# Dividing the side work of an attention kernel over two steps, and spreading the ones-products of its softmax sums

## The chip, the cores and the metric

The kernel runs on one core of one Trainium2 chip. The metric is the device time of one execution in microseconds (us). The median of three runs before the change is 3438.81 us.

## The reference, cut to what matters

Eight graphs ("frames") of 2048 nodes with 256 channels go through one attention layer with an adjacency mask, eight heads of 32 channels, a feed-forward part, and three layer norms:

```
qkv = einsum('fnc,ck->fnk', x, w_qkv); q, k, v = split(qkv, 3)      # F=8, N=2048, C=256, H=8, D=32
scores = einsum('fnhd,fmhd->fhnm', q, k) / sqrt(D)
scores = where(adj > 0, scores, -1e9)
attn = softmax(scores, axis=-1)
t = einsum('fhnm,fmhd->fnhd', attn, v).reshape(F, N, C)
x1 = layernorm(x + t)
h = relu(x1 @ w1 + b1)
out = layernorm(x + layernorm(x1 + h @ w2 + b2))
```

All data is float32.

## The kernel before, in words

**Steps and groups.** The list `items` has 1024 entries (f, qc, g, mb): frame, chunk of 512 queries, one of two halves of the heads (four heads each), and one of 16 blocks of 128 keys. The main loop takes one item per *step*. The 16 steps of one (f, qc, g) are a *group*; there are 64 groups, eight to a frame. At step t the program issues, in this order: at most one piece of *side work* (`advance`), the exponentials of item t+1, the scores of item t+2, the values product of item t, and the adding-up of item t. I call the place between the values product of one step and the scores of the next step the *slot* of that step.

**What a step holds on each engine.** TensorE (PE): four score matmuls, one for each head (L215), and four values matmuls (L234). VectorE (DVE): two additions of the mask to the scores, which also move them out of PSUM (L218). ScalarE (ACT): one exponential over 128x2048 (L222). The scores live in three PSUM tiles `s0` to `s2`; a step takes two of them in turn, so the scores of the next step need the first mask addition of this one.

**The sums of the softmax** are not made by the matmul that makes the values. The 16 exponential tiles of a group are first added: blocks 0, 3, 6, 8, 11, 13, 15 by GpSimd (POOL, L256, six additions), blocks 1, 4, 7, 10 and 2, 5, 9, 12 in two chains by accumulating DMAs that POOL issues (L253, six DMAs of 1 MB; each waits for the one before it in its chain), and block 14 stays alone. Then `denominator` multiplies the four remaining tiles by ones (L292): four sets of four matmuls, in the order block 14, first chain, second chain, POOL's tile. It runs inside the next group: two sets in the slot of block 3 and two in the slot of block 4. Then come a copy (L294), four transposes (L299) and reciprocals on DVE (L304 to L306).

**The rest of the side work** are generators in the list `fill`, sorted by due time. `turn` transposes the rows of the next frame and makes its queries (L152, L172), `project` makes its keys (L172) and values (L197), `outcome` divides by the sums (L328), and `tail` does layer norm, feed-forward (L394, L405, L415), layer norm, residual and layer norm, with bn_stats on DVE (L263, L264), scaling on ACT (L274) and products on POOL (L397, L399, L339, L341). A generator yields a positive number to sleep so many steps, or `BANK` when it wants the one free PSUM bank (of `x0` and `x1` one holds the running output of the group, the other serves side work). `advance(t, 1)` grants one `BANK` per step; after a grant the generator runs to its next yield, so a whole piece is issued in one slot: two matmuls of 128x512 for L172 or L405, eight of 128x128 for L197, four of 128x256 for L415, eight for L292, four transposes for the others. The first step of a group gets no slot.

**POOL's queue** runs in program order: L256, L253 and the tail's instructions stand in it as their steps issued them. A chain DMA that has to wait for the DMA before it holds up everything behind it.

Of the kernel before, what the change touches and what calls it, by code (L numbers as in the profile page):

```python
# [10 lines left out]
F32 = mybir.dt.float32  # L11
# [8 lines left out]
P = 128  # L20
H = 8
D = 32
CH = 512
# [3 lines left out]

SUM_MIN = 1e-25
SUM_MAX = 1e19
BANK, TURNED, ROOM, INPUTS = -1, -2, -3, -10  # L30

MASKED = -57344.0
CODE = -5.0
# [22 lines left out]
def fast_path(ctx, tc, cst, x, adj, out, RS):  # L56
    nc = tc.nc
    F, N, C = x.shape
# [18 lines left out]
    ctx.enter_context(tc.manual_schedule())  # L77

    ident, identb, wqkv, w1s, w2s = cst["ident"], cst["identb"], cst["wqkv"], cst["w1s"], cst["w2s"]
    state = {"pair": 0, "side": None, "turn": 0, "turned": False, "tails": 0}  # L80

    def score_pair():
        i = state["pair"]
# [57 lines left out]

    def queries(f, c, xT):
        for g in range(2):
            yield BANK
            QT[f, c, g] = channels(qp, "qT", xT, g * P)

    def turn_rows(xc, xT):
        for a in range(2):
# [17 lines left out]
        yield from queries(f, c, xT)  # L166
        give(xT)

    def channels(pool, name, xT, k0):
        ps = bank()  # L170
        for a in range(2):
            nc.tensor.matmul(ps, wqkv[:, a, k0:k0 + P], xT[:, a, :], start=(a == 0), stop=(a == 1))  # L172
        t = pool.tile([P, CH], F32, name=name)
        nc.scalar.copy(t, ps)
        return t

    def reload(f, c):
        while (f, c) not in XT:
# [7 lines left out]
    def project(f, c, g, xT=None):  # L186
        if xT is None:
            xT = yield from reload(f, c)
            while len(KT) < (2 * f + g) * NCK + c:
                yield 1  # L190
        yield BANK
        KT[f, c, g] = channels(kp, "kT", xT, C + g * P)
        yield BANK
        ps = bank()
        for j in range(TPC):
            for a in range(2):
                nc.tensor.matmul(ps[:, j * P:(j + 1) * P], xT[:, a, j * P:(j + 1) * P],  # L197
                                 wqkv[:, a, 2 * C + g * P:2 * C + (g + 1) * P], start=(a == 0), stop=(a == 1))
        v = vp.tile([P, TPC, P], F32, name="v")
        nc.scalar.copy(v, ps.rearrange("p (j c) -> p j c", c=P))  # L200
        V[f, c, g] = v
        give(xT)
# [21 lines left out]
    LAST = MB - 1  # L224
# [19 lines left out]
    ALONE = 14  # L244

    ENDED = (13, 15)
    SUM = 4

    def add_up(item):
        f, qc, g, mb = item  # L250
# [29 lines left out]
    def denominator(f, qc, g):  # L280
        grp = (f, qc, g)
        terms = [PT.pop((f, qc, g, ALONE))] + [PT.pop((f, qc, g, chain[0])) for chain in MOVED + (POOLED,)]
        if (f, qc, g) == items[-1][:3]:
            terms[3:3] = [PT.pop((f, qc, g, b)) for b in ENDED]
        yield BANK
        ps = bank()
        for n, term in enumerate(terms):
            if n == 2:
                yield BANK
            for h in range(4):  # L290
                r = D * h
                nc.tensor.matmul(ps[r:r + D, :], cst["ones"], term[:, h, :], start=(n == 0), stop=(n == len(terms) - 1))  # L292
        dT = op.tile([P, CH], F32, name="dT")
        nc.scalar.copy(dT, ps)  # L294
        yield 1
        yield BANK
        ps = bank()
        for j in range(TPC):
            nc.tensor.transpose(ps[:, j * P:(j + 1) * P], dT[:, j::TPC], ident)  # L299
        if g == 0:  # L300
            RC[f, qc] = op.tile([P, TPC, H], F32, name="rc")
        rc = RC[f, qc]
        den = ps.rearrange("p (j c) -> p j c", c=P)[:, :, ::D]
        nc.vector.reciprocal(rc[:, :, 4 * g:4 * g + 4], den)  # L304
        nc.vector.tensor_tensor(RS[:, 0], RS[:, 0], den, ALU.add)
        nc.vector.tensor_tensor(RS[:, 1], RS[:, 1], den, ALU.min)  # L306
        if g == 1:
            begin = items.index((f, qc, g, LAST)) + SUM + 2
            start(begin, outcome(f, qc) if (f, qc) != (F - 1, NCK - 1) else finish(f, qc), begin)

    def outcome(f, qc):
        yield ROOM
        state["tails"] += 1
        xin = x[f, qc * CH:(qc + 1) * CH, :].rearrange("(p j) c -> p j c", p=P)
        y = yp.tile([P, TPC, C], F32, name="y")
        yield from divide(f, qc, y)
        nc.gpsimd.dma_start(y, xin, accum_op=ALU.add)
        begin = items.index((f, qc, 1, LAST)) + SUM + 2
        start(begin + 10, tail(f, qc, y, xin), begin + 26)

    def divide(f, qc, y):
        rc = RC.pop((f, qc))
# [63 lines left out]
    def feed_forward(y):  # L386
        yield TURNED
        state["turned"] = True
        yT = work.tile([P, 2, CH], F32, name="turned")
        for a in range(2):  # L390
            yield BANK
            ps = bank()
            for j in range(TPC):
                nc.tensor.transpose(ps[:, j * P:(j + 1) * P], y[:, j, a * P:(a + 1) * P], ident)  # L394
            nc.scalar.activation(yT[:, a, :], ps, AF.Identity, bias=cst["be1c"][:, a:a + 1], scale=cst["g1c"][:, a:a + 1])
        yield 1
        nc.gpsimd.tensor_tensor(y, y, rows(cst["g1r"]), ALU.mult)  # L397
        yield 1
        nc.gpsimd.tensor_tensor(y, y, rows(cst["be1b2r"]), ALU.add)  # L399
        hT = work.tile([P, 2, CH], F32, name="hT")  # L400
        for d in range(2):
            yield BANK
            ps = bank()
            for a in range(2):
                nc.tensor.matmul(ps, w1s[:, a, d * P:(d + 1) * P], yT[:, a, :], start=(a == 0), stop=(a == 1))  # L405
            nc.scalar.activation(hT[:, d, :], ps, AF.Relu, bias=cst["b1s"][:, d:d + 1], scale=1.0)
        state["turned"] = False
        yield 1
        z = y
        for jj in range(0, TPC, 2):  # L410
            yield BANK
            ps = bank()
            for j in range(jj, jj + 2):
                for d in range(2):
                    nc.tensor.matmul(ps[:, (j - jj) * C:(j - jj + 1) * C], hT[:, d, j * P:(j + 1) * P], w2s[:, d, :],  # L415
                                     start=(d == 0), stop=(d == 1))
            nc.vector.tensor_tensor(z[:, jj:jj + 2, :], ps.rearrange("p (b c) -> p b c", c=C), z[:, jj:jj + 2, :], ALU.add)
# [4 lines left out]
    def start(t, gen, due):  # L422
        fill.append([t, gen, 1, due])
        fill.sort(key=lambda e: e[3])

    def advance(t, banks):
        inputs = True
        for e in list(fill):  # L430
            while e[0] <= t:
                if e[2] == BANK:
                    if not banks:
                        break
                    banks -= 1
                elif e[2] < INPUTS:
                    inputs = inputs and not any(u is not None for u in live[:INPUTS - e[2]])
                    if not inputs:
                        break
                elif e[2] == TURNED and state["turned"] or e[2] == ROOM and state["tails"] == 2:  # L440
                    break
                e[2] = next(e[1], None)
                if e[2] is None:
                    fill.remove(e)
                    break
                if e[2] > 0:
                    e[0] = t + e[2]

    items = [(f, qc, g, mb) for f in range(F) for qc in range(NCK) for g in range(2) for mb in range(MB)]
    LEAD = 2  # L450

# [61 lines left out]
    for t, (f, qc, g, mb) in enumerate(items):  # L513
        if mb == 0 and t:
            state["side"] = 1 - state["side"]
        if g == 1 and mb % 2 and (f + 1 < F or qc + 1 < NCK):
            load_mask(f + (qc + 1) // NCK, (qc + 1) % NCK, mb // 2)
        if f + 1 < F:
            for what, *which in NEXT.get((2 * qc + g, mb), []):
                due = t + MB // 2 if what is turn else items.index((f + 1, 0, which[1], which[0] * TPC)) - LEAD - 1  # L520
                start(t, what(f + 1, *which), due)
        if t == len(items) - MB // 2:
            state["rows"] = take([P, TPC, C], F32)
            nc.sync.dma_start(state["rows"], x[f, qc * CH:(qc + 1) * CH, :].rearrange("(p j) c -> p j c", p=P))
        if mb:
            advance(t, 1)

        if t + 1 < len(items):
            exponentials(items[t + 1])
        if t + LEAD < len(items):  # L530
            nf, _, ng, nmb = items[t + LEAD]
            t0 = t
            while (nf, nmb // TPC, ng) not in V:
                advance(t0, 1)
                t0 += 1
            scores(items[t + LEAD])
        values(items[t])
        add_up(items[t])
        if mb == LAST:
            start(t + SUM, denominator(f, qc, g), t)  # L540
    t = len(items)
    state["side"] = None
    while fill:
        t += 1
        advance(t, 1)


@with_exitstack
# [233 lines left out]
```

## Time and profile before

| what | value |
|---|---|
| three timed runs | 3435.35, 3440.09, 3438.81 us |
| the profiled execution: its own time | 3440.89 us |
| its span in the trace | 3439.1 us |
| busy DVE / ACT / POOL | 2731.0 / 2426.5 / 2586.7 us |
| DVE L218 mask additions | 2048, 1219 ns each |
| ACT L222 exponentials | 1024, 1911 ns each |
| POOL L256 additions | 382, 4898 ns each |
| first values product / end of the span | 94.86 / 3439.1 us |

The page counts an engine as busy while an instruction is in its pipeline; on PE neighbouring matmuls overlap, so the timeline's starts tell more than the durations. A matmul in float32 shows as two records. In the arrows, `[0.41 <-DVE p L218]` behind a row means that its engine was idle for 0.41 us before it, until the DVE instruction of line 218 had released it.

### The profile page before, as it was taken

The numbers are of one execution on the slowest core, as the hardware profiler recorded it, in microseconds if no ns is written. First come the engines' busy times: TensorE is split into PE (matmuls) and PEld (weight loads), VectorE is DVE, ScalarE is ACT, GpSimd is POOL, SyncE is SP. The second block draws the span as 40 slices with busy tenths as digits, with TensorE's granted clock in tenths as the row PEclk, the third lists the DMA queues.
The fourth block names the chain that finished last, engine by engine and source line by source line (L and its number), as shares of the span: only waits on it lengthen the run. The fifth ranks groups of instructions, "written<-read, shape, count | busy, mean of one in ns | idle before, by whom it ended". The sixth has DMA issues, their size and how long they took to land. (4 is left out here: it accounts for less than half of the span.)

```text
span 3439.1 us, 54435 instructions
## 1 busy us (share of the span) xinstructions
PE 3179.1 (92%) x22036; PEld 1038.5 (30%) x22036; DVE 2731.0 (79%) x3203; ACT 2426.5 (71%) x1937; POOL 2586.7 (75%) x1357
## 2 busy tenths in 40 slices
PE   6989999999999999999999999999999999998995
PEld 5222332223322233222332323223332223322222
DVE  4788768887788877888788887888768887689885
ACT  3677767776677767777677776777767777677774
POOL 0577768887688776888678876787777877788885
PEclk8999999999999999999999999999999999999998
DMA  8678768778678777778777777687776787777774
GB/s 309 149 156 173 173 161 174 158 159 200 142 167 184 154 180 153 163 172 181 170 154 170 161 175 178 141 180 172 164 179 140 160 187 167 169 158 154 151 162 99
DMA packets 149298, 575.99 MB, mean 167 GB/s; under 512 B 14608, under 2 KB 67344, under 8 KB 99888
## 3 DMA queue, kind: packets, MB, share of 16 engines
q0 software_dynamic: 64560, 435.85, 63.2%
q1 hardware_dynamic: 83664, 135.30, 11.4%
q8 instruction: 174, 2.85, 0.3%
q10 hardware_dynamic: 816, 1.31, 0.1%
q14 instruction: 84, 0.69, 0.1%
HBM read 131.99 MB, written 37.75 MB: 49 GB/s over the span
## 5 line engine op out<-in xcount | busy, mean ns | idle before, releaser
L218 DVE TENSOR_TENSOR p<-s,mask 128x1024 f32<-128x1024 f32 x2048 | 2410.0, 1219 | 568.5 <-PE s L215 343.9
L222 ACT ACTIVATE p<-p 128x2048 f32<-128x2048 f32 x1024 | 1956.6, 1911 | 484.6 <-DVE p L218 371.2
L256 POOL TENSOR_TENSOR p<-p 128x2048 f32<-128x2048 f32 x382 | 1851.8, 4898 | 385.9 <-ACT p L222 383.4
L215 PE MATMUL s<-qT,kT 32*128 32x512 f32 x8192 | 1169.8, 641 | 184.9 <-DVE p L218 174.6
L234 PE MATMUL x<-p,v 128*32 128x512 f32 x8192 | 1091.8, 605 | 2.3 <-ACT p L222 2.3
L253 POOL DMA_DIRECT2D p<-p x384 | 385.6, 1024 | 376.0 <-DMA p<-p 188.4
L215 PEld LDWEIGHTS s<-qT,kT 32*128 32x128 f32 x8192 | 320.5, 183 | 822.3 <-DVE p L218 756.2
L234 PEld LDWEIGHTS x<-p,v 128*32 128x32 f32 x8192 | 161.1, 108 | 780.1 <-issue 211.5
L172 PE MATMUL x<-in,wqkv 128*128 128x512 f32 x472 | 235.2, 621 | 14.7 <-DMA in<-xd 14.1
L292 PE MATMUL x<-p,ones 128*32 128x512 f32 x2064 | 244.9, 592 | 1.9 <-DMA p<-p 1.9
L274 ACT ACTIVATE y<-y,nb,rs 128x256 f32<-128x256 f32 x372 | 219.0, 590 | 7.1 <-POOL nb L271 7.1
L263 DVE BATCH_NORM_STATS2 st<-y 128x6 f32<-128x256 f32 x372 | 155.4, 418 | 0.0
L172 PEld LDWEIGHTS x<-in,wqkv 128*128 128x128 f32 x472 | 80.2, 189 | 170.9 <-issue 112.7
L294 ACT COPY dT<-x 128x512 f32<-128x512 f32 x64 | 37.4, 585 | 126.3 <-PE x L292 126.3
L415 PE MATMUL x<-w2s,hT 128*128 128x256 f32 x504 | 125.5, 392 | 0.1
L405 PE MATMUL x<-turned,w1s 128*128 128x512 f32 x248 | 123.0, 618 | 0.0
L197 PEld LDWEIGHTS x<-wqkv,in 128*128 128x128 f32 x896 | 104.2, 191 | 47.0 <-issue 41.1
L197 PE MATMUL x<-wqkv,in 128*128 128x128 f32 x896 | 114.9, 281 | 0.0
L292 PEld LDWEIGHTS x<-p,ones 128*32 128x32 f32 x2064 | 66.8, 110 | 156.4 <-issue 151.0
L415 PEld LDWEIGHTS x<-w2s,hT 128*128 128x128 f32 x504 | 90.6, 189 | 62.0 <-issue 50.3
L268 POOL TENSOR_TENSOR rs<-rs,mhalf 128x4 f32<-128x4 f32 x93 | 96.2, 1035 | 7.8
L200 ACT COPY v<-x 128x512 f32<-128x512 f32 x58 | 33.9, 585 | 93.6 <-PE x L197 93.6
(114 smaller groups left out, 1467.6 us busy)
## 6 DMA issues: line engine op xcount, KB each, us to landing
p<-p POOLq DMA_DIRECT2D x384, 1024.0 KB, 10.1
mask<-md SPq DMA_DIRECT2D x248, 128.0 KB, 6.2
y<-in_x_dram POOLq DMA_DIRECT2D x62, 512.0 KB, 6.1
in<-xd SPq DMA_DIRECT2D x59, 512.0 KB, 10.9
p<-in_adj_dram SPq DMA_DIRECT2D x16, 1024.0 KB, 9.6
out_dram<-y SPq DMA_DIRECT2D x31, 512.0 KB, 6.4
in<-in_x_dram SPq DMA_DIRECT2D x29, 512.0 KB, 10.4
xd<-in SPq DMA_DIRECT2D x28, 512.0 KB, 9.2
```

What stands on the lines that cost most here:

```text
L172: nc.tensor.matmul(ps, wqkv[:, a, k0:k0 + P], xT[:, a, :], start=(a == 0), stop=(a == 1))
L197: nc.tensor.matmul(ps[:, j * P:(j + 1) * P], xT[:, a, j * P:(j + 1) * P], wqkv[:, a, 2 * C + g * P:2 * C + (g + 1) * P], start=(a == 0), s ...
L215: nc.tensor.matmul(ps2[half][:, j, :], KT[f, mb // TPC, g][r:r + D, (mb % TPC) * P:(mb % TPC + 1) * P], QT[f, qc, g][r:r + D, :], start=Tr ...
L218: nc.vector.tensor_tensor(pt[:, 2 * half:2 * half + 2, :], ps, MK[f, qc, mb // 2][:, mb % 2, None, :].to_broadcast([P, 2, CH]), ALU.add)
L222: nc.scalar.activation(PT[item], PT[item], AF.Exp, scale=1.0 / math.sqrt(D))
L234: nc.tensor.matmul(O[grp][r:r + D, :], V[f, mb // TPC, g][:, mb % TPC, r:r + D], PT[item][:, h, :], start=(mb == 0), stop=(mb == LAST))
L253: nc.gpsimd.dma_start(PT[f, qc, g, chain[0]], PT.pop(item), accum_op=ALU.add)
L256: nc.gpsimd.tensor_tensor(first, first, PT.pop(item), ALU.add)
L263: nc.vector.bn_stats(st, t[:, j, :])
L274: nc.scalar.activation(t[:, j, :], t[:, j, :], AF.Identity, bias=nb[:, j:j + 1], scale=rs[:, j:j + 1])
L292: nc.tensor.matmul(ps[r:r + D, :], cst["ones"], term[:, h, :], start=(n == 0), stop=(n == len(terms) - 1))
L415: nc.tensor.matmul(ps[:, (j - jj) * C:(j - jj + 1) * C], hT[:, d, j * P:(j + 1) * P], w2s[:, d, :], start=(d == 0), stop=(d == 1))
```

## The change

1. Pieces of two halves (L172 queries and keys, L197, L405, L415) get a `yield MORE` in their middle: the first half runs in one slot, the second in the next step's slot, with the PSUM bank held between them. While a piece is held nobody else gets a bank. If some other generator waits for a bank and is due within eight steps (`SOON`), the held piece is finished at once. It is also finished at once in the last step of a group.
2. The ones-products are offered singly: one set of four matmuls, `MORE`, one set, `HOLD`, one set, `MORE`, one set. `HOLD` is not shortened by a due job, `MORE` is. They begin at block 1 of the next group instead of block 3 (`SUM` 2 instead of 4). Their due time and that of `outcome` become 0, ahead of all else.
3. Small moves: `project` is due seven steps earlier, `tail` may begin three steps earlier (13 steps after the group's last, `2 + 4 + 7`, against 16, `4 + 2 + 10`), and `outcome` at the same step as before.

```
-    def channels(pool, name, xT, k0):
+    def channels(store, pool, name, key, xT, k0):
+        yield BANK
         ps = bank()
         for a in range(2):
+            if a:
+                yield MORE
             nc.tensor.matmul(ps, wqkv[:, a, k0:k0 + P], xT[:, a, :], start=(a == 0), stop=(a == 1))
...
     def project(f, c, g, xT=None):
...
         for j in range(TPC):
+            if j == TPC // 2:
+                yield MORE
             for a in range(2):
                 nc.tensor.matmul(ps[:, j * P:(j + 1) * P], xT[:, a, j * P:(j + 1) * P],
...
-    SUM = 4
+    SUM = 2
...
     def denominator(f, qc, g):
...
         for n, term in enumerate(terms):
-            if n == 2:
-                yield BANK
+            if n:
+                yield HOLD if n == 2 else MORE
             for h in range(4):
...
         if g == 1:
-            begin = items.index((f, qc, g, LAST)) + SUM + 2
-            start(begin, outcome(f, qc) if (f, qc) != (F - 1, NCK - 1) else finish(f, qc), begin)
+            begin = items.index((f, qc, g, LAST)) + SUM + 4
+            start(begin, outcome(f, qc) if (f, qc) != (F - 1, NCK - 1) else finish(f, qc), 0)
...
-        begin = items.index((f, qc, 1, LAST)) + SUM + 2
-        start(begin + 10, tail(f, qc, y, xin), begin + 26)
+        begin = items.index((f, qc, 1, LAST)) + SUM + 4
+        start(begin + 7, tail(f, qc, y, xin), begin + 26)
...
     def feed_forward(y):
...
             for a in range(2):
+                if a:
+                    yield MORE
                 nc.tensor.matmul(ps, w1s[:, a, d * P:(d + 1) * P], yT[:, a, :], start=(a == 0), stop=(a == 1))
...
             for j in range(jj, jj + 2):
+                if j > jj:
+                    yield MORE
                 for d in range(2):
...
-    def advance(t, banks):
+    def resume(e, t):
+        e[2] = next(e[1], None)
+        state["holder"] = e if e[2] in (MORE, HOLD) else None if state["holder"] is e else state["holder"]
+        if e[2] is None:
+            fill.remove(e)
+        elif e[2] > 0:
+            e[0] = t + e[2]
+
+    def advance(t, free=True, finish=False):
         inputs = True
+        if state["holder"]:
+            free = False
+            resume(state["holder"], t)
         for e in list(fill):
-            while e[0] <= t:
+            while e[2] is not None and e[0] <= t and e is not state["holder"]:
                 if e[2] == BANK:
-                    if not banks:
+                    if not free:
                         break
-                    banks -= 1
+                    free = False
...
-                e[2] = next(e[1], None)
-                if e[2] is None:
-                    fill.remove(e)
-                    break
-                if e[2] > 0:
-                    e[0] = t + e[2]
+                resume(e, t)
+        late = any(e[2] == BANK and e[0] <= t and e[3] <= t + SOON for e in fill)
+        while state["holder"] and (finish or late and state["holder"][2] == MORE):
+            resume(state["holder"], t)
+
+    SOON = 8
...
-                due = t + MB // 2 if what is turn else items.index((f + 1, 0, which[1], which[0] * TPC)) - LEAD - 1
+                due = t + MB // 2 if what is turn else items.index((f + 1, 0, which[1], which[0] * TPC)) - LEAD - 8
...
-            advance(t, 1)
+            advance(t, finish=mb == LAST)
...
-            start(t + SUM, denominator(f, qc, g), t)
+            start(t + SUM, denominator(f, qc, g), 0)
```

More of the change, by code (lines that the diff above doesn't have):

```diff
@@ L29 @@
 SUM_MAX = 1e19
-BANK, TURNED, ROOM, INPUTS = -1, -2, -3, -10
+BANK, MORE, HOLD, TURNED, ROOM, INPUTS = -1, -2, -3, -4, -5, -10
 MASKED = -57344.0
@@ L79, in fast_path @@
     ident, identb, wqkv, w1s, w2s = cst["ident"], cst["identb"], cst["wqkv"], cst["w1s"], cst["w2s"]
-    state = {"pair": 0, "side": None, "turn": 0, "turned": False, "tails": 0}
+    state = {"pair": 0, "side": None, "turn": 0, "turned": False, "holder": None, "tails": 0}
     def score_pair():
@@ L143, in queries @@
         for g in range(2):
-            yield BANK
-            QT[f, c, g] = channels(qp, "qT", xT, g * P)
+            yield from channels(QT, qp, "qT", (f, c, g), xT, g * P)
     def turn_rows(xc, xT):
@@ L167, in turn @@
         give(xT)
-    def channels(pool, name, xT, k0):
+    def channels(store, pool, name, key, xT, k0):
+        yield BANK
         ps = bank()
         for a in range(2):
+            if a:
+                yield MORE
             nc.tensor.matmul(ps, wqkv[:, a, k0:k0 + P], xT[:, a, :], start=(a == 0), stop=(a == 1))
-        t = pool.tile([P, CH], F32, name=name)
-        nc.scalar.copy(t, ps)
-        return t
+        store[key] = pool.tile([P, CH], F32, name=name)
+        nc.scalar.copy(store[key], ps)
     def reload(f, c):
@@ L190, in project @@
                 yield 1
-        yield BANK
-        KT[f, c, g] = channels(kp, "kT", xT, C + g * P)
+        yield from channels(KT, kp, "kT", (f, c, g), xT, C + g * P)
         yield BANK
@@ L287, in denominator @@
         for n, term in enumerate(terms):
-            if n == 2:
-                yield BANK
+            if n:
+                yield HOLD if n == 2 else MORE
             for h in range(4):
@@ L533, in fast_path @@
             while (nf, nmb // TPC, ng) not in V:
-                advance(t0, 1)
+                advance(t0, finish=True)
                 t0 += 1
@@ L544, in fast_path @@
         t += 1
-        advance(t, 1)
+        advance(t, finish=True)
 @with_exitstack
```

## The prediction

> **What bounds the kernel now.** I read the page first, then the groups of instructions, the waits, the timeline of PE and that of POOL. Page and groups:
>
> ```profile
> PE 3179.1 (92%) x22036; PEld 1038.5 (30%) x22036; DVE 2731.0 (79%) x3203; ACT 2426.5 (71%) x1937; POOL 2586.7 (75%) x1357
> L215 PE MATMUL s<-qT,kT 32*128 32x512 f32 x8192 | 1169.8, 641 | 184.9 <-DVE p L218 174.6
> p<-p POOLq DMA_DIRECT2D x384, 1024.0 KB, 10.1
> ```
>
> PE is the fullest engine, and nearly all of its later idle time stands before the score matmuls, ended by the mask addition. The waits say how often, and show a second thing, POOL held up by its own chain DMAs:
>
> ```profile
> POOL p L253 <- DMA p<-p: 188.4, 43, 6.2
> PE s L215 <- DVE p L218: 174.6, 359, 1.5
> ```
>
> (Columns: us in all, times, longest.) PE waited 359 times; there are 357 steps without side work in the order of PE's instructions, so the idle time is that of the empty slots. The timeline of PE over five steps (start, length, instruction):
>
> ```profile
> 1634.47 1.07 PE L234 MATMUL x<-p,v 128*32 128x512 f32 x8
> 1635.94 1.14 PE L215 MATMUL s<-qT,kT 32*128 32x512 f32 x8 [0.41 <-DVE p L218]
> 1637.02 1.06 PE L234 MATMUL x<-p,v 128*32 128x512 f32 x8
> 1638.01 1.99 PE L415 MATMUL x<-w2s,hT 128*128 128x256 f32 x8
> 1639.93 1.14 PE L215 MATMUL s<-qT,kT 32*128 32x512 f32 x8
> 1641.01 1.07 PE L234 MATMUL x<-p,v 128*32 128x512 f32 x8
> 1642.00 2.05 PE L197 MATMUL x<-wqkv,in 128*128 128x128 f32 x16
> 1643.98 1.14 PE L215 MATMUL s<-qT,kT 32*128 32x512 f32 x8
> 1645.05 1.06 PE L234 MATMUL x<-p,v 128*32 128x512 f32 x8
> 1645.94 1.90 PE L292 MATMUL x<-p,ones 128*32 128x512 f32 x16
> 1647.77 1.14 PE L215 MATMUL s<-qT,kT 32*128 32x512 f32 x8
> 1648.84 1.06 PE L234 MATMUL x<-p,v 128*32 128x512 f32 x8
> ```
>
> From one L234 to the next is one step. Scores cost 1.07 us and values 1.00, so PE alone needs 2.07. An empty step takes 2.55, a step with a whole piece of L415 3.99, of L197 4.04, of ones 3.79. A whole piece hides DVE completely; an empty step waits 0.4 to 0.5 us for it. Cutting the whole timeline at the L234 starts gives the same by kind: whole L172 or L405 3.98, L415 3.99, L197 4.05, two ones-sets 3.78, transposes 2.65 to 2.86, empty steps other than a group's first 2.60 on average.
>
> The third view is POOL's timeline at the end of a second-half group whose sums fall in the group starting at 1535.18:
>
> ```profile
> 1514.99 0.93 POOL L253 DMA_DIRECT2D p<-p  x1 [0.28 <-issue]
> 1521.20 0.87 POOL L253 DMA_DIRECT2D p<-p  x1 [5.28 <-DMA p<-p]
> 1521.77 4.87 POOL L256 TENSOR_TENSOR p<-p 128x2048 f32<-128x2048 f32 x1
> 1526.26 2.71 POOL L397 TENSOR_TENSOR y<-y,g1r 128x1024 f32<-128x1024 f32 x1
> 1528.58 1.23 POOL L253 DMA_DIRECT2D p<-p  x1
> 1529.19 3.00 POOL L399 TENSOR_TENSOR y<-y,be1b2r 128x1024 f32<-128x1024 f32 x1
> 1531.51 9.82 POOL L256 TENSOR_TENSOR p<-p 128x2048 f32<-128x2048 f32 x2
> ```
>
> The last row ends at 1541.33 with the group's last addition. Its ones-product is the fourth set and runs at about 1548.7, 7 us later: POOL has room now.
>
> **What the Trainium skill says.** "Perfetto Trace Analysis", Optimization Strategy: where the most-contended engine changes over time, interleaving the regimes may help. The trace agrees that there are two regimes, PE-bound steps of 3.98 and DVE-bound steps of 2.55. "DMA: Bandwidth & Descriptors", Issuing engines are not separate DMA queues: all DMAs interleave on the same 16 engines. Here the chain DMAs land 6.8 to 13.9 us after issue (median 10.1), so their landing isn't a constant. "GPSIMD Engine Reference", Elementwise, has 4497 ns for an addition over 2048 floats; the trace shows 4.5 us from start to start of two such additions, so POOL's additions are at their price and won't shrink.
>
> **Part 1, the spreading on PE.** No matmul is added or removed. I counted the slots in the instruction order of both programs. Before: 357 empty, 126 of two ones-sets, 118+62 whole L172 and L405, 61 L415, 56 L197. After: 160 empty; ones 104 single and 74 double; L172 168 halves and 34 whole; L405 44 and 40; L415 64 and 29; L197 14 and 49. So 84+22+32+7 = 145 pieces are divided, 52 ones-pairs are, and 197 empty slots vanish. Transposes stay.
>
> What a half costs isn't in the trace. A whole L172 piece takes 1.91 us of PE (step 3.98 less 2.07); its four weight loads follow each other by 0.43, so 4 x 0.43 = 1.72 are streaming and 0.2 is paid once for each entry. A half is 0.86 + 0.2 = 1.06, its step 3.13. Bounds: 3.03 if the 0.2 is halved too, 3.2 if DVE or ACT makes the shorter step late. I take 3.13. Each divided piece then saves 3.98 + 2.60 - 2 x 3.13 = 0.32, in all 145 x 0.32 = 46. A single ones-set has the shape of the values product and its pair costs 1.71 over 2.07, so a single costs 0.86, step 2.93; 52 x (3.78 + 2.60 - 2 x 2.93) = 52 x 0.52 = 27. Sum: 73 us gained, of the 174.6 of idle. With the bounds 102 (290 halves x 0.10 more) to 53 (290 x 0.07 less).
>
> **Part 2, what DVE and ACT give back.** A step's two mask additions occupy DVE 2.36 us, a bn_stats with its aggregate 0.60 more. A half-filled step of 3.13 carries one such pair (2.96) at no cost. But the feed-forward is now stretched, and in the order of instructions the norms of two tails meet: once in each frame four successive steps, with empty slots, have two pairs each. DVE then needs 3.56 against 2.60, 3.8 us of backlog in four steps. Up to about 1.1 is free: the steps with L299 already run DVE 3.45 (additions 2.35, pair 0.6, L304 to L306 0.5) in 2.75 without growing. So 2.7 is lost there, and by the same count 0.5 and 0.8 in two other groups of a frame: 4.0 for seven frames, 6.6 in the last, 35 at most; part is absorbed in longer steps behind. ACT gets two or three L274 (0.59) in one step where it had one, after the same norms; exponentials end 0.5 to 2.6 us before their product, which covers most: 0 to 5. I take 30 together, bounds 10 and 40.
>
> **Part 3, the ones-products earlier.** In 26 groups the four sets go singly into the slots of blocks 1 to 4, the last at the same block as before. In 37 groups, mostly those behind a second-half group, a due job makes them two pairs in blocks 1 and 2: the second chain and POOL's sum are wanted two steps earlier, about 5 us net of the longer step at block 1. For the group shown: slot 2 would begin near 1540.0 and the fourth set near 1540.9, while POOL ends at 1541.33. So the room of 7 us becomes 0.4 of stall, and all of PE stands behind that matmul. Also the second-half groups get shorter (51.8 to about 49 by the prices above) while POOL's work in them doesn't. I walked POOL's queue step by step with 4.53 per addition, 0.6 per DMA issue, 2.3 per tail product and one landing time; with 11.0 us of landing this hits the observed ends of the last addition before within about 1 us. In the new order the same walk has the fourth set late by about 3 us a frame; with 10.5 it is about 1, with 11.2 about 5. I take 20 us in all, bounds 5 and 45. The landing time decides, and denser steps bring the chain DMAs closer together.
>
> **Moves priced at nothing.** `outcome` starts at the same step; `project` and `tail` only gain time. SP's loads of masks and inputs keep their steps. Holding the bank over two steps costs nothing by itself, since nobody else is granted one. In the first frame the wait for `in<-xd` (14 us in all) may shrink, up to 10.
>
> **Sum.** 3440.9 (the profiled execution, 2.1 above the median of the runs) - 73 + 30 + 20 = 3418, and I leave it so.
>
> **Rivals.** (a) The gain comes whole: DVE's and POOL's lateness vanishes in the buffers. For it: DVE is only 79% busy, POOL 75%. Against it: the two meetings above are local. 3440.9 - 73 = 3368. (b) Slower: the ones-products at blocks 1 and 2 wait for the DMA chains. Three landings in series per chain, with POOL's queue standing still behind each, are what the 188.4 us of waits show; if landings grow to about 12 us with the denser steps, POOL falls behind in every group. At 2 us for each of the 37 pairs, 74 more than nothing: 3440.9 - 73 + 30 + 74 = 3472. It decides from (73 - 30)/37 = 1.2 us a pair on. Against it: a stall also gives POOL time to catch up. (c) The change does little, because pieces that fall due are finished whole: 74 of 178 ones-slots are still double. Against it: 197 of 357 empty slots go. About 3439.
>
> **How the numbers follow.** My forecast has 0.50, (a) 0.20, (b) 0.24, (c) 0.06. A difference under 0.2% (7 us) can't be told from none here. Faster: (a) 0.20 and 0.41 of the forecast; same: 0.06 of the forecast, (c) 0.06 and 0.02 of (b); slower: 0.03 and 0.22. The forecast's own range is 3395 to 3445; to leave no more than two in ten out the range takes (a)'s centre and half of (b): 3362 to 3462.
>
> **What would show it.** Right: the wait of L215 for L218 falls by some 80 us; half steps of about 3.13; new waits of L292 for DMA or POOL, at most 1 us a group on average; and L218 behind two bn_stats pairs in one group of each frame. Wrong: half steps well above 3.13, which would mean that the switch to another stationary shape costs more than 0.2; or L292 waiting above 1.2 us for each pair, with chain landings of 12 us and more.

## The result and the profile after

The changed kernel takes 3568.25 us (median of four runs, 3566.44 to 3571.08), the kernel before, beside it, 3437.78. The ratio is 1.038, 95% interval 1.0362 to 1.0398: 130 us slower, where 20 us faster was forecast. The profiled execution took 3566.44 us, its span is 3564.6.

Page of the changed kernel (PE's busy time, then groups of instructions; behind the second bar the idle time before the group and what ended it):

```profile
PE 3241.4 (91%) x22036; PEld 1030.7 (29%) x22036; DVE 2739.5 (77%) x3203; ACT 2434.7 (68%) x1937; POOL 2584.9 (73%) x1357
L217 PE MATMUL s<-qT,kT 32*128 32x512 f32 x8192 | 1190.0, 651 | 179.2 <-DVE p L220 176.2
L294 PE MATMUL x<-p,ones 128*32 128x512 f32 x2064 | 269.7, 613 | 66.9 <-POOL p L258 47.2
L265 DVE BATCH_NORM_STATS2 st<-y 128x6 f32<-128x256 f32 x372 | 154.5, 415 | 64.8 <-DMA y<-in_x_dram 64.8
```

(Lines have moved by two or more: L217 is L215 of before, L220 is L218, L258 is L256, L265 is L263, L294 is L292.) The number of instructions is the same. The ones-products of the kernel before, in the same columns:

```profile
L292 PE MATMUL x<-p,ones 128*32 128x512 f32 x2064 | 244.9, 592 | 1.9 <-DMA p<-p 1.9
```

Its bn_stats waited for no DMA at all, so two kinds of wait are new. The wait of the scores for the mask addition is as long as before, but of another kind. Waits of the changed kernel (us in all, times, longest):

```profile
PE s L217 <- DVE p L220: 176.2, 196, 10.3
...
DVE st L265 <- DMA y<-in_x_dram: 64.8, 8, 9.5
...
PE x L294 <- POOL p L258: 47.2, 23, 3.3
```

359 waits of at most 1.5 us have become 196, some of 10 us. The spreading itself does what it should. Timeline of PE in a stretch of divided L415 pieces (now L421), the step counted from L236 to L236:

```profile
1501.82 1.06 PE L236 MATMUL x<-p,v 128*32 128x512 f32 x8
1502.82 1.13 PE L421 MATMUL x<-w2s,hT 128*128 128x256 f32 x4
1503.88 1.14 PE L217 MATMUL s<-qT,kT 32*128 32x512 f32 x8
1504.95 1.06 PE L236 MATMUL x<-p,v 128*32 128x512 f32 x8
```

A half piece stands in 1.06 us and its step takes 3.13, with no wait. Cut at the values products, the median half step is 3.12 (L174, L409), 3.13 (L421) or 3.15 (L199), a single ones-set 2.92, an empty step 2.55. The time went elsewhere. Timeline of the changed kernel at the end of the fifth group of a frame, DVE, POOL and PE (start, length, instruction, idle time before it):

```profile
1619.62 0.68 DVE L331 TENSOR_TENSOR y<-x,rc 128x512 f32<-128x512 f32 x1
...
1620.60 0.87 POOL L319 DMA_DIRECT2D y<-in_x_dram  x1 [0.67 <-DVE y L331]
...
1622.56 1.06 PE L236 MATMUL x<-p,v 128*32 128x512 f32 x8
...
1631.89 0.43 DVE L265 BATCH_NORM_STATS2 st<-y 128x6 f32<-128x256 f32 x1 [9.32 <-DMA y<-in_x_dram]
1632.35 0.18 DVE L266 BATCH_NORM_AGGREGATE mv<-st 128x2 f32<-128x6 f32 x1
1632.45 2.33 DVE L220 TENSOR_TENSOR p<-s,mask 128x1024 f32<-128x1024 f32 x2
1633.71 2.09 PE L217 MATMUL s<-qT,kT 32*128 32x512 f32 x8 [10.09 <-DVE p L220]
...
1635.73 1.70 PE L236 MATMUL x<-p,v 128*32 128x512 f32 x8
```

The division (L331) ends at 1620.3. The DMA that adds x into y is issued at 1620.6. The next DVE instruction in program order that isn't a mask addition already under way is the tail's bn_stats on that same y: DVE stands for 9.32 us, the mask additions stand behind it, and PE stands for 10.09. This step takes 13.17 us, from 1622.56 to 1635.73. And when PE returns, the scores take 2.09 us where they take 1.14 elsewhere. The windows of the same place (length in us; busy us and instructions of PE, its weight loads, DVE, ACT and POOL; granted clock, DMA share, GB/s):

```profile
1614.80:1622.60 7.80, 6.75 (x56) 2.41 (x55) 7.36 (x8) 4.75 (x4) 6.51 (x8) 1.00 1.06 255
1622.60:1633.70 11.10, 1.02 (x12) 0.11 (x8) 1.78 (x4) 2.40 (x2) 7.93 (x2) 0.69 0.68 138
1633.70:1640.50 6.80, 6.79 (x44) 1.67 (x48) 5.89 (x7) 4.69 (x4) 0.00 (x0) 0.75 0.06 19
```

The clock is granted in full before the stall, 0.69 in it and 0.75 in the 7 us behind it: the stall costs more than its length. Such a stall stands at this place in six of the eight frames, the second to the seventh, and once in the seventh group of the first. The other new wait, PE at the ones-products of the seventh group of a frame:

```profile
1688.58 1.04 PE L294 MATMUL x<-p,ones 128*32 128x512 f32 x8
1690.56 1.06 PE L294 MATMUL x<-p,ones 128*32 128x512 f32 x8 [0.94 <-DMA p<-p]
...
1693.06 1.06 PE L236 MATMUL x<-p,v 128*32 128x512 f32 x8
1695.97 1.06 PE L294 MATMUL x<-p,ones 128*32 128x512 f32 x8 [1.85 <-DMA p<-p]
1699.62 1.93 PE L294 MATMUL x<-p,ones 128*32 128x512 f32 x8 [2.58 <-POOL p L258]
1701.48 2.09 PE L217 MATMUL s<-qT,kT 32*128 32x512 f32 x8
```

The sets for the first chain, the second chain and POOL's sum each come too early, and the scores behind them again run at half speed. Summed by place over the kernel, the steps stand 198 us above the prices of their kinds (15 us in the kernel before): 56 of it in the last step of the fifth group of the frames, 82 in the second pair of ones-sets of the first, fifth and seventh groups. I call the first cause, VectorE behind a bn_stats that waits for the DMA, A, and the second, the ones-products that come too early, B. C is the rival that divided pieces cost more than they save.

### The profile page after: what moved, and what is told of

The parts are those of the page before. It is cut to its first block, busy times and chain, and to the rows that moved or that the text cites. A ratio compares the mean times of both kernels' runs of the same rounds, so it can differ in the third digit from the quotient of the medians.

```text
span 3564.6 us, 54376 instructions
## 1 busy us (share of the span) xinstructions
PE 3241.4 (91%) x22036; PEld 1030.7 (29%) x22036; DVE 2739.5 (77%) x3203; ACT 2434.7 (68%) x1937; POOL 2584.9 (73%) x1357
## 5 line engine op out<-in xcount | busy, mean ns | idle before, releaser
L220 DVE TENSOR_TENSOR p<-s,mask 128x1024 f32<-128x1024 f32 x2048 | 2409.0, 1218 | 632.1 <-PE s L217 422.8
L258 POOL TENSOR_TENSOR p<-p 128x2048 f32<-128x2048 f32 x382 | 1813.1, 4746 | 403.4 <-ACT p L224 400.8
L217 PE MATMUL s<-qT,kT 32*128 32x512 f32 x8192 | 1190.0, 651 | 179.2 <-DVE p L220 176.2
L236 PE MATMUL x<-p,v 128*32 128x512 f32 x8192 | 1106.6, 613 | 2.9 <-ACT p L224 2.9
L255 POOL DMA_DIRECT2D p<-p x384 | 376.4, 1002 | 380.3 <-DMA p<-p 164.7
L217 PEld LDWEIGHTS s<-qT,kT 32*128 32x128 f32 x8192 | 325.0, 186 | 782.0 <-DVE p L220 687.3
L236 PEld LDWEIGHTS x<-p,v 128*32 128x32 f32 x8192 | 162.0, 108 | 796.3 <-issue 345.1
L294 PE MATMUL x<-p,ones 128*32 128x512 f32 x2064 | 269.7, 613 | 66.9 <-POOL p L258 47.2
L174 PE MATMUL x<-in,wqkv 128*128 128x512 f32 x472 | 257.7, 640 | 0.0
L265 DVE BATCH_NORM_STATS2 st<-y 128x6 f32<-128x256 f32 x372 | 154.5, 415 | 64.8 <-DMA y<-in_x_dram 64.8
L341 POOL TENSOR_TENSOR y<-y,g2r 128x1024 f32<-128x1024 f32 x31 | 75.8, 2447 | 77.7 <-ACT y L276 77.7
L421 PE MATMUL x<-w2s,hT 128*128 128x256 f32 x496 | 132.1, 398 | 0.0
L294 PEld LDWEIGHTS x<-p,ones 128*32 128x32 f32 x2064 | 63.8, 111 | 234.8 <-issue 125.9
L409 PE MATMUL x<-turned,w1s 128*128 128x512 f32 x248 | 128.9, 628 | 0.0
L174 PEld LDWEIGHTS x<-in,wqkv 128*128 128x128 f32 x472 | 73.4, 189 | 187.8 <-issue 161.1
L199 PEld LDWEIGHTS x<-wqkv,in 128*128 128x128 f32 x896 | 104.7, 191 | 53.6 <-ACT y L276 24.3
L199 PE MATMUL x<-wqkv,in 128*128 128x128 f32 x896 | 116.7, 282 | 0.0
L421 PEld LDWEIGHTS x<-w2s,hT 128*128 128x128 f32 x496 | 86.5, 189 | 86.0 <-issue 57.9
## 6 DMA issues: line engine op xcount, KB each, us to landing
p<-p POOLq DMA_DIRECT2D x384, 1024.0 KB, 10.2
```

The costliest lines, as they stand in the source:

```text
L217: nc.tensor.matmul(ps2[half][:, j, :], KT[f, mb // TPC, g][r:r + D, (mb % TPC) * P:(mb % TPC + 1) * P], QT[f, qc, g][r:r + D, :], start=Tr ...
L220: nc.vector.tensor_tensor(pt[:, 2 * half:2 * half + 2, :], ps, MK[f, qc, mb // 2][:, mb % 2, None, :].to_broadcast([P, 2, CH]), ALU.add)
L236: nc.tensor.matmul(O[grp][r:r + D, :], V[f, mb // TPC, g][:, mb % TPC, r:r + D], PT[item][:, h, :], start=(mb == 0), stop=(mb == LAST))
L255: nc.gpsimd.dma_start(PT[f, qc, g, chain[0]], PT.pop(item), accum_op=ALU.add)
L258: nc.gpsimd.tensor_tensor(first, first, PT.pop(item), ALU.add)
```

## The experiments

All are the changed kernel or parts of it. The kernel before ran beside each call and took 3447 to 3450 us there, 3438 beside the changed kernel, so ratios to it are compared, not times alone.

**The wait for the residual taken away.**

```
-        nc.gpsimd.dma_start(y, xin, accum_op=ALU.add)     # in outcome
```

> The changed kernel with the accumulating DMA of x into y in outcome left out, so the first residual is missing from the output; the order of all other instructions stays. Theory A (most of the loss is VectorE standing behind a bn_stats that waits for this DMA, because the division now comes so late that the tail starts in its wake): the wait of bn_stats for the DMA (64.8 us) goes, and with it the 13 us steps at the end of one group in each frame and their half-clock aftermath; about 3568 - 75 = 3493. Rival B (the loss is the ones-products waiting for GpSimd and the chain DMAs): little change, 3555 or more, apart from a lighter DMA load. Rival C (divided pieces cost more on TensorE than they save): no change.

Measured: 3495.47 us, ratio 1.0134 (1.0117 to 1.0151), against 1.038. The bn_stats waits are gone but for one of 8.3 us near the end of the kernel, behind another DMA; the last step of the fifth group fell from 56 us above its price to 2, and most of the ones-waits stayed (56.1 us of 66.9 on PE). The order of all else in the program was the same, so A is worth 2.5%, with the effect of a lighter DMA load in it, which this run can't separate. B remains.

**The ones-products from block 3 again.**

```
-    SUM = 2
+    SUM = 4
-            begin = items.index((f, qc, g, LAST)) + SUM + 4
+            begin = items.index((f, qc, g, LAST)) + SUM + 2
```

The second change is made in both places where the line stands.

> The changed kernel with the ones-products begun at block 3 again (SUM 4, the other starts kept at the same steps), still offered singly. Theory B: the waits of the ones-products (66.9 us on TensorE and as much on its weight loads) vanish with their half-clock steps; the steps by kind cost 7 us more than in the changed kernel; about 3568 - 90 = 3478. Theory A alone: its 13 us steps stay, since the divisions still fall at blocks 12 and 13 of that group; 3560 to 3575 if B is nothing. C: no change.

Measured: 3566.92 us, ratio 1.0335 (1.0313 to 1.0357), a miss by 90 us; by the time alone B would be nothing. But the ones-waits did vanish, while the divisions now came late in more groups, the first and the seventh, and the first cause took the place of the second:

```profile
PE s L217 <- DVE p L220: 228.7, 205, 8.8
...
DVE st L265 <- DMA y<-in_x_dram: 124.2, 23, 9.2
```

23 waits of bn_stats instead of 8. So moving one job shifts the divisions, and a test of B alone must hold them in place.

**Each part of the change alone.** First the ones-products alone: the four `yield MORE` of `channels`, `project` and `feed_forward` taken out.

> Only the ones-products part of the change: single sets from block 1, all other pieces whole. The divisions stand at blocks 5 to 6, so A can't occur. By kinds of steps it is 40 us under the kernel before. If early ones as such are the trouble (B in its simple form), 37 or more pairs wait 2 us each and it ends near 3438 - 40 + 80 = 3478; if they wait only because the stretched tails have shifted GpSimd's queue, near 3410.

Measured: 3440.25 us, ratio 0.9979 (0.9972 to 0.9986). Its ones-sets hardly wait: 9.4 us for POOL and 5.0 for DMA, PE and its weight loads together. So early ones as such aren't the trouble; they wait when the other pieces are divided as well. But 3440 is 30 us above the 3410 expected for that case. The gain of 40 us by kinds of steps came to 7: the rest is given back in small pieces over many places (57 us above the prices, 15 us of it whole key pieces at block 12, where PE waits 9.2 us for the input load `in<-xd`, as it does for 14.1 us in the kernel before), and what delays the others stays open.

Then the dividing alone: ones-products in two pairs at blocks 3 and 4 (`if n == 2: yield BANK`, `SUM = 4`).

> Only the dividing of pieces: ones-products in two pairs at blocks 3 and 4 as before. By kinds of steps 51 us under the kernel before. A predicts that its 13 us steps stay (divisions at blocks 12 and 13 in one group of a frame): 3438 - 51 + 75 + 17 for coinciding bn_stats = about 3480. C (divided pieces dear): half steps over 3.2 us and no such single long steps. B: no ones-waits, so 3438 - 51 + 17 = about 3405 if A is nothing.

Measured: 3519.28 us, ratio 1.02 (1.0182 to 1.0218). The long steps of A are there (56 us in the last step of the fifth group, bn_stats waits of 57.9 us in 7 places), half steps are 3.12, so C falls. It is 40 us slower than A's number: divisions that come late stall in other places too, 24 us at block 9 of the seventh group among them. There the timeline of waits names the output DMA whose y the division overwrites.

**The division kept in time by a third y buffer.** A division waits (`yield ROOM`) while two tails are under way. Divided pieces make the tails longer.

```
-    yp = ctx.enter_context(tc.tile_pool(name="yp", bufs=2))
+    yp = ctx.enter_context(tc.tile_pool(name="yp", bufs=3))
-    qp ... bufs=2 * NCK + 2      # likewise vp
+    qp ... bufs=2 * NCK + 1
-                elif e[2] == TURNED and state["turned"] or e[2] == ROOM and state["tails"] == 2:
+                elif e[2] == TURNED and state["turned"] or e[2] == ROOM and state["tails"] == 3:
```

> The changed kernel with a third y buffer and room for three tails (two of the q and v tiles given up for the space). The division then needn't wait for an older tail and falls at blocks 4 to 7; the slots hold the same kinds of pieces as in the changed kernel, and nothing is left out. Theory A with its cause (the stretched feed-forward keeps both tail places, the division comes late, the tail's bn_stats follows its DMA at once): the bn_stats wait of 64.8 us falls under 10, time about 3568 - 75 = 3493. Theory B says that the ones-waits stay, 60 us or more. Rival (fewer q and v tiles, or three tails at once, cost as much as they save): 3550 or more.

Measured: 3455.17 us, ratio 1.0011 (0.9997 to 1.0024), 38 us better than expected. That is 3.7% under the changed kernel, with nothing left out and the same count of empty slots. It is more than e1 gave (2.5%); the waits of the division for an output DMA (9.0 us) and of PE for the division (6.0 us) went with it, and the rest of the difference is not taken apart. The divisions stand at blocks 5 to 7 again. The ones-waits stayed, at the same place as before; they now stand alone:

```profile
PE x L294 <- POOL p L258: 41.5, 23, 3.5
DVE st L265 <- DMA y<-in_x_dram: 8.7, 1, 8.7
```

POOL's timeline of this kernel in the group before such a pair, and the fourth ones-set on PE:

```profile
1613.77 2.17 POOL L255 DMA_DIRECT2D p<-p  x1
1624.23 0.85 POOL L255 DMA_DIRECT2D p<-p  x1 [8.30 <-DMA p<-p]
1624.81 4.87 POOL L258 TENSOR_TENSOR p<-p 128x2048 f32<-128x2048 f32 x1
1629.34 2.66 POOL L399 TENSOR_TENSOR y<-y,g1r 128x1024 f32<-128x1024 f32 x1
1631.65 1.20 POOL L255 DMA_DIRECT2D p<-p  x1
1632.24 3.02 POOL L401 TENSOR_TENSOR y<-y,be1b2r 128x1024 f32<-128x1024 f32 x1
1634.56 9.78 POOL L258 TENSOR_TENSOR p<-p 128x2048 f32<-128x2048 f32 x2
```

```profile
1644.39 1.78 PE L294 MATMUL x<-p,ones 128*32 128x512 f32 x8 [3.45 <-POOL p L258]
1646.10 2.07 PE L217 MATMUL s<-qT,kT 32*128 32x512 f32 x8
```

POOL stands 8.30 us before a chain DMA until the one before it has landed, and from there to 1644.34 it has no gap: the last addition ends 0.05 us before the fourth set starts. It is the queue that the prediction walked, with a longer stop at its head than the 5.28 us of the kernel before.

**Both.** The third y buffer and `SUM = 4` together.

> The same with the ones-products begun at block 3. With A and B both as I read them, the single long steps are gone, and what remains is the table of steps: 66 us under the kernel before, and about 20 us given back where the bn_stats of two tails meet: 3442 - 66 + 20 = about 3396, that is 1.2 to 1.4% faster than the kernel before. If the ones-products still wait over 20 us, B is not only their early start; if it ends near 3440 or above, something else than A and B eats the table's gain.

Measured: 3393.88 us, ratio 0.9827 (0.9795 to 0.9859). The time is the number that was expected; the ratio, 1.7% faster than the kernel before, is somewhat better than the 1.2 to 1.4% expected, since the kernel before took 3450 us beside this call, not the 3442 from which the expectation was worked out. Waits and groups of this kernel:

```profile
PE s L217 <- DVE p L220: 121.2, 188, 1.6
...
DVE st L265 <- DMA y<-in_x_dram: 7.8, 4, 5.4
```

```profile
L294 PE MATMUL x<-p,ones 128*32 128x512 f32 x2064 | 254.4, 596 | 0.0
```

No long wait of the scores, no wait of the ones-products on PE. The step from e5 to e6 is 1.8%, which is B with the divisions held in place; of the 60 us between their profiled executions, 13 lie behind the last values product and 47 before it. The order of the kernel before has its divisions at blocks 6 and 7 wherever one falls, so a third buffer had nothing to hasten there; that control wasn't run on the chip.

**The third buffer with a whole feed-forward, and without.** Without: the two `yield MORE` of `feed_forward` taken out, `SUM = 4`, two y buffers.

> The changed kernel with the feed-forward's pieces (w1, w2) whole again and the ones-products from block 3, two y buffers as before. The tails are then as short as before in slots, the divisions fall at blocks 6 to 10. By kinds of steps 44 us under the kernel before. A: bn_stats still follows the DMA closely in one group of a frame, so some 20 to 30 us of its wait may remain; 3442 - 44 + 25 = about 3423. If only the feed-forward's stretching matters, 3400.

Measured: 3466.11 us, ratio 1.0045 (1.0032 to 1.0058), a miss by 43 us: bn_stats still waited 52.5 us in 16 places, since the divisions at blocks 9 and 10 (in the first and fifth groups of most frames) are still close before the tail's fixed start at block 12. So dividing the feed-forward isn't alone in holding the places of the tails. With the third buffer:

> The third y buffer, the ones-products from block 3, and the feed-forward's pieces whole: the kernel of e7 with one thing changed, the room for a third tail. Theory A: e7's waits of bn_stats for the DMA (52.5 us) go, and with them most of its 83 us above the table; about 3466 - 60 = 3406. Rival (the third buffer does nothing by itself, e6 was fast for its divided feed-forward): 3450 or more.

Measured: 3405.22 us, ratio 0.9871 (0.9854 to 0.9887), as expected; 1.7% for the buffer alone, with bn_stats waiting 6.3 us and the divisions at blocks 6 to 9. Dividing the feed-forward may be worth another 0.4% once its harm is gone (e6 against e9), but their intervals touch.

**The tail tied to its DMA.** e6, with the tail begun no sooner than eight steps after the DMA.

```
         nc.gpsimd.dma_start(y, xin, accum_op=ALU.add)
+        yield 8
         begin = items.index((f, qc, 1, LAST)) + SUM + 2
```

> The third-y kernel with the ones-products from block 3, and the tail begun eight steps after its DMA instead of at a fixed step. By kinds of steps 15 us under the same kernel without the delay (144 empty slots against 179), and steps with the bn_stats of two tails fall from 66 to 39. If those two are what is left, 3394 - 15 - 8 = about 3371 to 3380; if GpSimd's queue or the ones-products fall behind again, 3394 or more.

Measured: 3377.11 us, ratio 0.979 (0.9773 to 0.9806), as expected and the fastest version, 2.1% under the kernel before, though its interval touches that of e6. The gain over e6 isn't the wait of bn_stats for the DMA, which was already down to 7.8 us there (here one wait of 14.9 us is left, 10 us before the end of the kernel). What changed is what was expected: 35 empty slots fewer, and the four long steps where two tails meet are gone, 3.13 or less instead of 3.36.

## Why the prediction was wrong

**What held.** The price of a half piece (3.13 predicted, 3.12 to 3.15 found), of a single ones-set (2.93; 2.92) and the counts of the table; e6, whose own table has 66 us, less 20 for the tails that meet, came out within 2 us of that sum. The meeting of two tails' bn_stats was real and close in size. Of the four steps in the third group of a frame, the first on PE, with the wait that ends it:

```profile
1513.75 1.06 PE L236 MATMUL x<-p,v 128*32 128x512 f32 x8
1516.04 1.14 PE L217 MATMUL s<-qT,kT 32*128 32x512 f32 x8 [1.22 <-DVE p L220]
1517.11 1.06 PE L236 MATMUL x<-p,v 128*32 128x512 f32 x8
```

3.36 a step against 2.55, four times in each of six frames (2.83 in the first and the last), 3.2 us where 2.7 was taken. The sign of "the wait of L215 for L218 falls by some 80 us" failed because A's stalls bear the same name: without them it fell by 48 in e1, 65 in e5, 53 in e6 and 83 in e8, which also lacks the meeting. One reading was wrong, without weight: the 14.1 us of waits for `in<-xd` aren't in the first frame but in the first seven, and they are gone in the changed kernel.

**The step that failed.** "`outcome` starts at the same step; `project` and `tail` only gain time", priced at nothing. `outcome` is started at the same step, but it then waits for `ROOM`, and a tail stretched by divided pieces holds its place longer. The division fell to blocks 12 and 13 in the fifth group of six of the eight frames (blocks 6 and 7 before), which could be read from the slots that I had counted (the transposes of the division stand there in the order of PE's instructions). The tail's start is a fixed step and had been moved three steps nearer. So bn_stats was issued one step behind a DMA on whose landing, first before and then after, the trace says:

```profile
DMA to landing us min/median/max: 5.4/5.7/6.9
DMA to landing us min/median/max: 5.2/6.3/11.4
```

And it was issued on an engine on which every score of the kernel waits. I counted the pieces by kind and didn't ask what waits for which. "Holding the bank over two steps costs nothing by itself, since nobody else is granted one" belongs to the same step: whoever isn't granted a bank comes later, and a late tail keeps its place. e7 and e9 point to that, since a third place helps with a whole feed-forward too. The move that seemed to give time took the distance away. Worth 2.5% by e1, 3.7% by e5, with what else the third buffer takes away. How much of it the tail's earlier start is worth by itself was not run.

**The term that was too small.** 20 us, bounds 5 and 45, for the ones-products at blocks 1 and 2. The mechanism and the groups were right; it is 1.8% of the time, some 63 us, by e5 and e6. PE's own waits at the ones-products are 66.9 us, 1.8 for each of the 37 pairs, above the 1.2 from which rival (b) was to decide. So (b) had this wait nearly right at 2 us a pair, and its 3472 still lay 96 us under the time measured, because A was in no rival. Its sign was a landing time of 12 us; the median landing is 10.2 against 10.1. What grew is single stops: eight of 7.9 to 8.5 us in e5 at block 12 of the sixth or eighth group, such as the 8.30 us above, against 6.2 us at most before. On top of the waits comes the half-speed clock behind stalls, which the forecast has no term for: once under way, 3.4 us of the loop of the kernel before ran at half clock, 137 us of the changed kernel's, 37 of e5's, 7 of e6's.

The end of the kernel is 17 us longer as well (from the last values product on, 71.7 us against 54.5); its ones-sets wait 3.88 us for a chain there and a norm half 7.00 (1.91 and 5.39 before). What ends last in both is the tail of the chunk before the last. Its last residual DMA is issued 55.8 us after the last values product, against 32.4 before, so this tail comes later too. No run tests that.

## What to carry to other kernels

When pieces of work are stretched, look at what is held while they run (a buffer, a place among the allowed two), and at who waits for it; then look at starts that are fixed to a step and so no longer know when their input is issued. An instruction that waits for a DMA must not stand in the queue of an engine that feeds the critical loop: tie its start to the issue of the DMA, or keep the DMA in time. Here one buffer more turned 3.8% lost into 0.1% lost, and with the ones-products back at block 3 into 1.7% gained. A tied start without the third buffer was not run.

## What the runs showed of the hardware

A stall of PE of some 10 us costs more than itself. The granted clock falls to half within it and stays so for some microseconds after: 0.69 and 0.75 in the two windows above, scores of 2.09 us instead of 1.14. Once under way, the loop of the changed kernel has 22 such stretches at half clock, each 3.4, 6.8 or 10.2 us long. Short stalls can bring them too: the shortest single wait of PE with one directly behind it is 1.81 us there, while one of 3.29 us in e6 has none, and every longer wait in the loops of all runs has one. Over the loop the granted clock was 0.98 against 1.00 before, and over the span 0.969 against 0.990. Many short waits of half a microsecond, 359 of them in the kernel before, cost no clock.
